# First transformer of a four-layer kernel: scores and P V as one run of narrow products, values as wide products, O turned in another order

## The chip, the cores and the metric

The kernel runs on one core of a Trainium2 chip. The metric is the device time of one launch in microseconds (us). Three launches of the kernel before took 3877.02, 3872.96 and 3869.68 us, with a median of 3872.96 us.

## The reference

Four layers are chained on `x` of 4 x 512 tokens with 128 features. Each layer normalises `x`, runs a mixer `s` and a gate network `g`, and adds `s * silu(g)`. The gate network of the third layer (`L2_ffn`) is a transformer of six layers with 16 heads of 64 and a window of 32 keys; it is the "first transformer" of this change. The gate network of the fourth layer (`L3_ffn`) is a transformer of two layers with 8 heads and a window of 64; it shares code with the first.

```python
def attn_layer(x, Wqkv, qs, ksc, Wo):
    qkv = x @ Wqkv
    q, k, v = jnp.split(qkv, 3, -1)
    ...
    q = l2norm(q) * qs
    k = l2norm(k) * ksc
    q = q * cos * scale + rotate_half(q) * sin * scale
    k = k * cos * inv + rotate_half(k) * sin * inv
    out = local_attention(q, k, v)
    return out @ Wo
def local_attention(q, k, v):
    bk2, bv2 = (look(bk), look(bv))
    sim = jnp.einsum('bhwie,bhwje->bhwij', bq, bk2) * QK_SCALE
    sim = jnp.where(mask, -jnp.finfo(sim.dtype).max, sim)
    attn = jax.nn.softmax(sim, -1)
    return jnp.einsum('bhwij,bhwje->bhwie', attn, bv2)
```

`look` puts a block of 32 keys behind the block before it, so each block of 32 queries sees 64 keys. Each layer is followed by a feed-forward layer (norm, 128 to 2 x 341, GELU gate, back to 128).

## The kernel before

All matrices are fp32, with features on the 128 partitions and tokens along the row. `transformer` (line 705 on) runs three generators side by side: `queries_keys` (q and k of one batch row and one half of the heads), `attention`, and `feed_forward`. A batch row of a layer is a "row" here: six layers by four batch rows are 24 rows in the first transformer, and each row has two slots, one for each group of eight heads. `merge` (line 949) draws from the three generators by hand-written weights. Each `yield` names a cost, and the generator that has done the smallest share of its weight goes next. That fixes the order in which the program issues work; a scheduler behind it may still move an instruction whose inputs are late. [...]

A slot of attention has two units, `j` = 0 and 1, each with four heads, that is 16 blocks of 32 queries by 4 heads. A unit goes through these steps in `class _Transformer`:

- `scores` (line 1380 on): two wide bf16 products put the mask into a PSUM tile, then 64 narrow products (line 1402: 64 rows by 32 columns of the array, 64 keys) add q k. After half of them, a `yield` lets the other generators in, and `turn` of the unit before is issued. VectorE then takes the row maximum (line 1415), subtracts it in two instructions (line 1419) and, after ScalarE's exponential (line 1424), sums the rows (line 1426) and takes the reciprocal (line 1428).
- `turn`: eight transposes bring P into a PSUM tile and ScalarE copies it out as `PT` (line 1440).
- `weigh`: 64 narrow products P V in two halves with a `yield` behind each; VectorE divides in two instructions (line 1473) into `On`.
- `turn_back`: eight transposes, and ScalarE copies the result in two instructions (line 1493) into `OT`. After the second unit of a slot four wide products with `Wo` follow (`l_OT,l_wo`), and VectorE adds to `y` (line 1533).
- `values`, once for each slot and one slot ahead: 16 products of 64 array columns by 256, in two halves of eight at different places, each copied out by ScalarE (line 1365) into `vo`; four DMAs on SP's queue (line 1369 on) make `ve`, a second copy in which every other block is shifted by one block.

`PS` is a pool of four PSUM tiles, two banks each, that all three generators share (`S2()` and `M()`). q and k come from four wide products for each group (`l_wqk`) that ScalarE squares (line 1304) and VectorE multiplies by the tables twice (lines 1306 and 1308); POOL adds (lines 1305 and 1309); two wide products (`sqp`), a logarithm and an exponential give the unit length, and VectorE multiplies (line 1333); eight DMAs on SP's queue rearrange each tile.

In the profile an fp32 product shows as two matmul records, wide or narrow.

Of the kernel before, what the change touches and what calls it, by code (L numbers as in the profile page):

```python
# [16 lines left out]
F32 = mybir.dt.float32  # L17
BF16 = mybir.dt.bfloat16
AF = mybir.ActivationFunctionType
ALU = mybir.AluOpType  # L20
AX = mybir.AxisListType
# [3 lines left out]
B, S, D = 4, 512, 128  # L25
NTOK = B * S
NT = S // 128
# [11 lines left out]
class Net:  # L39
    def __init__(self, tc, ctx, a, out):  # L40
        self.tc, self.nc, self.a, self.out = tc, tc.nc, a, out
        self.ctx, nc = ctx, self.nc
        self.pool = lambda name, bufs=1, **kw: tc.tile_pool(name=name, bufs=bufs, reuse_waits="tile", **kw)
        enter = ctx.enter_context
        self.keep = enter(self.pool("keep"))
        self.small = enter(self.pool("small", 4))

        core = self.keep.tile([128, 384], F32, name="core")
        nc.scalar.dma_start(core, a["k_core"])
        self.ident = core[:, 0:128]  # L50
        self.mean = core[:, 128:256]
        self.flip = core[:, 256:384]
        self.cen = self.keep.tile([128, 128], F32, name="cen")
        nc.vector.tensor_tensor(self.cen, self.ident, self.mean, ALU.subtract)
        self.eps = self.keep.tile([128, 1], F32, name="eps")
        nc.vector.memset(self.eps, 1e-5)
        self.xn = self.keep.tile([128, NTOK], F32, name="xn")
        self.turn = 0
# [648 lines left out]
    def transformer(self, pre, depth, heads, window, consts):  # L707

        with ExitStack() as stack:
            pool = lambda name, bufs=1, **kw: stack.enter_context(self.pool(pre + name, bufs, **kw))
            pools = [pool("ps", 4, space=PSUM)]

            pools += [pool("c", side="right"), pool("tab", 3, side="right"), pool("w", side="right")]
            pools += [pool("qk", 4), pool("v", 2), pool("p", 2), pool("t", 2)]
            t = _Transformer(self, pre, heads, window, pools, consts)
            t.exp_tables()  # L720
            rows = [(l, b) for l in range(depth) for b in range(B)]
            passes = t.queries_keys(rows), t.attention(rows), t.feed_forward(rows)
            slots = len(rows) * t.GP
            for i in range(slots + t.GP + 2 + t.lag):
                run = []
                if i < slots:
                    run.append((until_none(passes[0]), 10.3))
                if 0 < i <= slots + 1 + t.lag:
                    run.append((until_none(passes[1]), t.attention_weight))
                if i >= t.GP + 2 + t.lag:  # L730
                    run.append((until_none(passes[2]), t.feed_forward_weights[i % t.GP]))
                merge(run)
# [448 lines left out]
class _Transformer:  # L1181
    def __init__(self, net, pre, heads, window, pools, consts):
        self.net, self.nc, self.a, self.pre = net, net.nc, net.a, pre
        self.heads, self.W, self.inner = heads, window, heads * 64
        self.GP = heads // 8
        self.NB = 128 // window
        self.split = self.NB == 4
        self.PS, C, self.TB, self.WT, self.QK, self.VP, self.PP, self.TP = pools
        nc, a = self.nc, self.a
        self.T = 4 if self.split else 2  # L1190
        self.NU = self.T * 64 // window
        self.cols = net.load(C, a[pre + "cols"], name=pre + "_cols")
        k = net.load(C, a[consts][:, 0:256], name=pre + "_k", queue=nc.scalar)
        self.ones, self.cen = k[:, 0:128], k[:, 128:256]
        self.tiny = C.tile([128, 1], F32, name=pre + "_tiny")
        nc.vector.memset(self.tiny, 1e-36)
        n = NT // self.T
        self.mask = C.tile([128, n, 512], BF16, name=pre + "_mask")
        nc.gpsimd.dma_start(self.mask, a[consts][:, 256 : 256 + 512 * n].rearrange("p (t n) -> p t n", t=n))
        self.identb = C.tile([128, 128], BF16, name=pre + "_identb")  # L1200
        nc.vector.tensor_copy(self.identb, net.ident)

        self.ve = [C.tile([128, self.NU, 1024 // self.NB], F32, name=f"{pre}_ve{i}") for i in range(2)]
        for i in range(2 if self.split else 1):
            for lo, hi in self.second():
                nc.gpsimd.memset(self.ve[i][lo:hi, 0, :], 0.0)
        self.made, self.shift, self.weights = {}, {}, {}

        self.attention_weight = 20.4 if self.split else 25.0
        self.feed_forward_weights = (7.7, 1.7) if self.GP == 2 else (9.4,)  # L1210


        self.lag = 1 if self.split else 0
        self.y = net.xn
# [367 lines left out]

def _constants():
    f = np.float32
    p = np.arange(128)[:, None]
    c = {}
    c["k_core"] = np.concatenate([np.eye(128), np.full((128, 128), 1.0 / 128), np.eye(128)[::-1]], 1)
    i, j, n = p % 32, np.arange(32)[None], np.arange(64)[None]  # L1590
    own, before = np.where(j <= i, 0.0, MASKED), np.where(j > i, 0.0, MASKED)
    odd = p // 32 % 2 == 1
    band = np.where(odd, np.concatenate([before, own], 1), np.concatenate([own, before], 1))
    first = np.where((p < 32) & (n >= 32), MASKED, band)
    lmask = [np.where(n <= (q * 128 + p) // 8, 0.0, MASKED) for q in range(NT)]
    c["k_l0_masks"] = np.concatenate([first, band, band, *lmask], 1)
    hm = (p // 8 == np.arange(16)[None]).astype(f)
    quarter = (p % 32 // 8 == np.arange(4)[None]).astype(f)
    hl = (p % 64 // 8 == np.arange(8)[None]) * f(0.125)
    c["k_l0"] = np.concatenate([hm, quarter, hl], 1)  # L1600
    tri = np.where(np.arange(128)[None] <= p, 0.0, NEG)
    c["k_causal"] = np.concatenate([np.zeros((128, 384)), -tri], 1)
    c["k_diff"] = np.concatenate([np.where(np.arange(128)[None] <= p, 0.0, MASKED), (p % 32 == 8).astype(f)], 1)
    c["k_half"] = (p // 16 % 2 == np.arange(2)[None]).astype(f)
    for name, t in (("l2", L2F), ("l3", L3F)):
        w = t["window"]
        ones = np.kron(np.eye(4), np.ones((32, 32)))
        cen = np.eye(128) - 1.0 / 128

        block, i = np.arange(128) // w, np.arange(128)[:, None] % w  # L1610
        j = np.arange(w)[None]
        mask = np.zeros((128, NT, 2, 2, w), f)
        for q in range(NT):
            for blk in range(128 // w):
                rows = block == blk
                own, before = (0, 1) if blk % 2 == 0 else (1, 0)
                mask[rows, q, :, own] = np.where(j <= i, 0.0, MASKED)[rows][:, None]
                seen = (j >= i) & (q + blk > 0)
                mask[rows, q, :, before] = np.where(seen, 0.0, MASKED)[rows][:, None]
        c["k_" + name] = np.concatenate([ones, cen, mask.reshape(128, -1)], 1)  # L1620
        c["k_rot_" + name] = _rotary(w // 2, w)
    return {k: np.ascontiguousarray(v, dtype=f) for k, v in c.items()}
# [32 lines left out]
    return np.stack(out, 1)  # L1655


def _halves(w, heads, even_first):

    n = heads * 64
    h, r, d = np.arange(heads // 4)[:, None, None], np.arange(4)[None, :, None], np.arange(32)[None, None]
    order = []
    for g in range(heads // 4):
        for i in range(2):
            for half in range(2):
                order.append((i * n + (4 * g + r) * 64 + 32 * half + d).reshape(-1))
    v = 2 * n + np.arange(n).reshape(heads // 8, 8, 64)
    for part in v:  # L1670
        order += [part[0::2].reshape(-1), part[1::2].reshape(-1)] if even_first else [part.reshape(-1)]
    return w[:, :, np.concatenate(order)]


def _layout(i):
# [19 lines left out]
    for pre, src, names in (  # L1695
        ("l2", "L2_ffn_", ("Wqkv", "Wo", "W1", "W2")),
        ("l3", "L3_ffn_", ("wqkv", "wo", "w1", "w2")),
    ):
        for dst, n in zip(("Wqkv", "Wo", "W1", "W2"), names):
            a[pre + dst] = i[src + n]  # L1700
        a[pre + "Wqkv"] = _halves(a[pre + "Wqkv"], (L2F if pre == "l2" else L3F)["heads"], pre == "l2")
        a[pre + "cols"] = _columns(*(i[src + n] for n in ("q_scale", "k_scale", "ln_g", "ln_b", "b1", "b2")))
    a["L3_attn_A"] = i["L3_attn_A"]

# [22 lines left out]
```

## Time and profile before

| What | Value |
|---|---|
| median of three launches | 3872.96 us |
| lowest, highest | 3869.68, 3877.02 us |
| span of the profiled execution | 3866.4 us |
| TensorE busy | 3490.9 us, 90% |
| VectorE busy | 2476.9 us, 64% |
| ScalarE busy | 1847.0 us, 48% |
| POOL busy | 1161.2 us, 30% |
| mean granted TensorE clock | 0.946 |
| first transformer | from 1566 us to 3330 us of the span |

The span runs from the first to the last instruction of one execution; it is 6.6 us below the median of the launches. The first transformer's last feed-forward instructions of each row (line 1579) stand 71.0 us apart in most rows (1925.4, 1996.4 and 2067.4 us, for example), and 72.5 to 76.1 us where a new layer begins. The busy share of TensorE is built from modelled ends, so the start of one group of products and the start of the next tell more than a duration.

### The profile page before, as it was taken

The numbers are of one execution on the slowest core, as the hardware profiler recorded it, in microseconds if no ns is written. First come the engines' busy times: TensorE is split into PE (matmuls) and PEld (weight loads), VectorE is DVE, ScalarE is ACT, GpSimd is POOL, SyncE is SP. The second block draws the span as 40 slices with busy tenths as digits, with TensorE's granted clock in tenths as the row PEclk, the third lists the DMA queues.
The fourth block names the chain that finished last, engine by engine and source line by source line (L and its number), as shares of the span: only waits on it lengthen the run. The fifth ranks groups of instructions, "written<-read, shape, count | busy, mean of one in ns | idle before, by whom it ended". The sixth has DMA issues, their size and how long they took to land.

```text
span 3866.4 us, 105326 instructions
## 1 busy us (share of the span) xinstructions
PE 3490.9 (90%) x46789; PEld 1892.2 (49%) x46917; DVE 2476.9 (64%) x3429; ACT 1847.0 (48%) x2508; POOL 1161.2 (30%) x994
## 2 busy tenths in 40 slices
PE   6886999899899999899999999999999999778887
PEld 4554455444444443454555555555555555445444
DVE  6675555411553351677888888888888887367765
ACT  3333666623133334455555555555555555445555
POOL 1001344400021113443443443443443342042220
PEclk7677999999899999999999999999999999889998
DMA  1000000001000000444334444444444434322221
GB/s 39 8 24 24 8 1 1 1 30 52 2 1 3 3 1 2 116 99 117 95 94 122 96 96 120 95 99 117 98 99 103 103 88 98 110 63 69 53 49 42
DMA packets 123574, 236.12 MB, mean 61 GB/s; under 512 B 29624, under 2 KB 44128, under 8 KB 117728
## 3 DMA queue, kind: packets, MB, share of 16 engines
q1 hardware_dynamic: 114064, 209.58, 22.1%
q10 hardware_dynamic: 8624, 19.29, 1.6%
q8 instruction: 369, 6.05, 0.7%
q0 software_dynamic: 432, 0.51, 0.1%
q14 instruction: 85, 0.70, 0.1%
HBM read 50.08 MB, written 5.54 MB: 14 GB/s over the span
## 4 chain that ended last, share of the span: by engine, by line
PE 69%; ACT 11%; DVE 9%; issue 6%; DMA 2%; POOL 2%; SPq 0%; DVEq 0%; POOLq 0%; ACTq 0%
PE S L122 45%; PE S L126 6%; PE M L122 5%; PE S L1402 4%; PE o L1104 4%; ACT l_P L581 3%; PE o L614 2%; ACT l_PT L1440 1%; DMA l_tab<-in_k_rot_l 1%; PE S L1014 1%; DVE l_mx L1079 1%; ACT l_P L1126 1%; DVE l_rot L1333 1%; PE M L741 1%; DVE l_rot L1306 1%
## 5 line engine op out<-in xcount | busy, mean ns | idle before, releaser
L1309 POOL TENSOR_TENSOR l_rot<-l_rot,rotp 128x1024 f32<-128x1024 f32 x224 | 527.5, 2364 | 285.9 <-DVE rotp L1308 219.2
L1305 POOL TENSOR_TENSOR sqp<-sqp 128x512 f32<-128x512 f32 x224 | 293.3, 1310 | 832.8 <-ACT sqp L1304 825.6
L122 PE MATMUL S<-hb,l_wqk 128*128 128x512 f32 x896 | 449.4, 621 | 36.7 <-ACT l_PT L1440 11.2
L1304 ACT ACTIVATE sqp<-S 128x1024 f32<-128x1024 f32 x224 | 229.5, 1025 | 319.2 <-PE S L122 318.0
L1333 DVE SCALAR_TENSOR_TENSOR l_rot<-S,l_rot 128x1024 f32<-128x1024 f32 x224 | 262.9, 1211 | 65.3 <-ACT S L1330 37.4
L1306 DVE TENSOR_TENSOR l_rot<-S,l_tab 128x1024 f32<-128x1024 f32 x224 | 272.1, 1215 | 50.0 <-ACT sqp L1304 46.6
L126 PE MATMUL S<-core,l_P 128*128 128x128 f32 x1856 | 265.2, 287 | 38.9 <-ACT l_P L1424 16.4
L126 PEld LDWEIGHTS S<-core,l_P 128*128 128x128 f32 x1856 | 215.0, 146 | 136.8 <-issue 45.8
L122 PE MATMUL S<-l_KT,l_QT 32*128 32x256 f32 (+7 forms) x1536 | 247.4, 475 | 34.7 <-ACT l_P L1126 14.5
L1126 ACT ACTIVATE l_P<-S 128x1024 f32<-128x1024 f32 x160 | 156.8, 1023 | 254.9 <-PE S L122 254.1
L1308 DVE TENSOR_TENSOR rotp<-S,l_tab 128x1024 f32<-128x1024 f32 x224 | 270.5, 1208 | 1.4 <-POOL l_rot L1309 1.3
L122 PEld LDWEIGHTS S<-hb,l_wqk 128*128 128x128 f32 x896 | 158.3, 192 | 224.7 <-issue 151.6
L122 PE MATMUL S<-sqp,l_k 128*128 128x512 f32 x448 | 226.5, 623 | 19.1 <-issue 7.2
L1402 PE MATMUL S<-l_qk 64*32 64x64 f32 (+1 forms) x13312 | 221.1, 230 | 19.4 <-DMA l_qk<-l_rot 1.9
L1079 DVE TENSOR_REDUCE l_mx<-S 128x2 f32<-128x768 f32 (+1 forms) x192 | 154.9, 863 | 123.8 <-PE S L1014 123.8
L1402 PEld LDWEIGHTS S<-l_qk 64*32 64x32 f32 (+1 forms) x13312 | 168.2, 108 | 134.0 <-issue 129.6
L1130 POOL TENSOR_SCALAR_AFFINE_SELECT l_P<-l_P 128x256 f32<-128x256 f32 x256 | 99.8, 408 | 405.5 <-ACT l_P L1126 398.5
L122 PE MATMUL S<-l_wv,hb 128*64 128x256 f32 (+1 forms) x1600 | 219.1, 395 | 2.4 <-ACT l_vo L1365 1.2
L122 PE MATMUL S<-l_OT,l_wo 128*128 128x512 f32 (+1 forms) x512 | 207.1, 544 | 8.0 <-DVE ffu L1571 7.9
L1415 DVE TENSOR_REDUCE mx<-S 128x16 f32<-128x1024 f32 (+1 forms) x128 | 155.7, 1216 | 89.9 <-PE S L1402 89.8
L122 PE MATMUL S<-hb,l_w 128*128 128x512 f32 (+1 forms) x384 | 189.6, 630 | 23.5 <-DVE hb L1559 14.1
L122 PEld LDWEIGHTS S<-l_ve,l_PT 64*32 64x32 f32 (+1 forms) x6656 | 159.9, 108 | 99.2 <-issue 70.5
(360 smaller groups left out, 6544.8 us busy)
## 6 DMA issues: line engine op xcount, KB each, us to landing
l_qk<-l_rot SPq DMA_DIRECT2D x896, 128.0 KB
l_ve<-l_vo SPq DMA_DIRECT2D x112, 256.0 KB
l_ve<-l_vo SPq DMA_DIRECT2D x96, 224.0 KB
l_tab<-in_k_rot_l ACTq DMA_DIRECT2D x16, 1024.0 KB
l_wqk<-in_l2Wqkv SPq DMA_DIRECT2D x12, 512.0 KB
l_wv<-in_l2Wqkv SPq DMA_DIRECT2D x12, 256.0 KB
l_wo<-in_l2Wo SPq DMA_DIRECT2D x12, 256.0 KB
l_ve<-l_vo SPq DMA_DIRECT2D x24, 128.0 KB
```

What stands on the lines that cost most here:

```text
L122: self.nc.tensor.matmul(out, lhsT, rhs, start=start, stop=stop)
L126: self.nc.tensor.transpose(out, in_, self.ident[:n, :n])
L1079: nc.vector.tensor_reduce(mxv[:, bs, 2 * m + e, 3 - i], s[u][:, :, c : c + n], axis=AX.X, op=ALU.max)
L1126: nc.scalar.activation(P[u], s[u], AF.Exp, scale=scale)
L1304: nc.scalar.activation(sq, p, AF.Square)
L1305: nc.gpsimd.tensor_tensor(sq[:, 0, :], sq[:, 0, :], sq[:, 1, :], ALU.add)
L1306: nc.vector.tensor_tensor(t[:, g], p, tab[:, 0], ALU.mult)
L1308: nc.vector.tensor_tensor(m, p, tab[:, 1], ALU.mult)
L1309: nc.gpsimd.tensor_tensor(t[:, g], t[:, g], m[:, ::-1, :], ALU.add)
L1333: nc.vector.scalar_tensor_tensor(t[:, g], p[:, g, :].unsqueeze(1).to_broadcast([128, 2, S]), 1e12, t[:, g], ALU.min, ALU.mult)
L1402: net.nc.tensor.matmul(sv[W * bl : W * bl + W, e, t, g, :].rearrange("p (s k) -> p s k", s=2), qk[0][r, g, j, W * c : W * c + W], kw, star ...
L1415: nc.vector.tensor_reduce(mx, flat, axis=AX.X, op=ALU.max)
```

## The change

A class `_Paired` takes the place of `_Transformer` where the window is 32. `queries_keys`, `feed_forward` and the second transformer keep their code.

- The 64 score products of a unit and the 64 P V products of the unit before are issued one after the other, with no `yield` between them. Two PSUM tiles are then in use, one for each.
- `values` is four wide products (128 columns by 512), the two halves in one iteration of the loop instead of two. The weights of V are no longer permuted on the host, and the four DMAs into `ve` have other slices of about the same sizes.
- `turn_back` writes its eight transposes in the order of `OT`, so one ScalarE copy of 128x1024 takes the place of two. The tokens in `OT` are then in another order, and the addition to `y` is two instructions of 256 columns instead of one of 512.
- The subtraction of the maximum is one instruction of 1024 columns instead of two of 512.
- The exponential, the row sum and the reciprocal are issued later: the exponential behind the first piece of `values` or of the `Wo` product, sum and reciprocal behind `turn`, which now comes at the end of the unit's own iteration.
- The mask is in the new order of the blocks, and the weight of attention in `merge` is 16.1 instead of 20.4.

```diff
-            t = _Transformer(self, pre, heads, window, pools, consts)
+            t = (_Paired if window == 32 else _Transformer)(self, pre, heads, window, pools, consts)
...
-        self.attention_weight = 20.4 if self.split else 25.0
+        self.attention_weight = 16.1 if self.split else 25.0
...
+class _Paired(_Transformer):
...
+    def values(self, u):
...
+        for m in (0, 2):
+            p = self.S2()
+            for n in range(2):
+                net.mm(p[:, n, :], hb[:, 128 * (m + n) : 128 * (m + n) + 128], w)
+            yield 1.72
+            nc.scalar.copy(vo[:, m : m + 2, :], p)
+        for lo in (0, 64):
+            nc.sync.dma_start(ve[lo : lo + 32], vo[lo : lo + 32])
+        nc.sync.dma_start(ve[96:128], vo[32:64])
+        nc.sync.dma_start(ve[32:64, 1:4, :], vo[96:128, 0:3, :])
...
+    def turn_back(self, u, OT):
+        net = self.net
+        t = self.S2().rearrange("p g (x q) -> p g x q", q=128)
+        for g in range(2):
+            for th in range(2):
+                for a in range(2):
+                    net.transpose(t[:, g, 2 * th + a, :], u["On"][:, a, 2 * th + g].rearrange("p e d -> p (e d)"))
+        ov = OT.rearrange("p (g j) n -> p j g n", j=2)
+        self.nc.scalar.copy(ov[:, u["j"]], t.rearrange("p g x q -> p g (x q)"))
...
+    def attention(self, rows):
...
+                s = self.scores(qk, u["j"])
+            if last:
+                o = self.weigh(last)
+            if u:
+                self.weights_of(u, s)
+            if last:
+                self.divide(last, o)
+            if u or last:
+                yield 2.8
+            behind = None
+            if i % 2 == 0 and i + 2 < len(units):
+                behind = self.values(units[i + 2])
+            elif i % 2 and i > 2:
+                behind = self.close(units[i - 2], OT.pop(i - 2))
+            if behind:
+                yield next(behind)
+            if u:
+                self.exponentials(u)
+            if behind:
+                yield from behind
+            if last:
...
+                self.turn_back(last, made)
+                yield 0.9
+            if u:
+                self.turn(u)
+                yield 0.9
```

## The prediction

> **What bounds the kernel now.** I read the page's slices first, then the first transformer by rows, then TensorE in order of time, then the chain of waits. Busy tenths and granted clock, in 40 slices of the span:
>
> ```profile
> PE   6886999899899999899999999999999999778887
> ...
> PEclk7677999999899999999999999999999999889998
> ```
>
> In slices 17 to 34, the first transformer, TensorE is near full. Two neighbouring rows of it (71.0 us each; columns are busy us of TensorE, its weight loads, VectorE, ScalarE, POOL, then clock, DMA share, GB/s):
>
> ```profile
> 1925.40:1996.40 71.00, 68.50 (x1243) 37.98 (x1248) 59.19 (x65) 38.83 (x44) 29.57 (x18) 1.00 0.40 94
> 1996.40:2067.40 71.00, 68.50 (x1243) 37.94 (x1248) 59.07 (x65) 38.83 (x44) 29.57 (x18) 1.00 0.39 92
> ```
>
> TensorE is the bound at 96%, VectorE has 83%, so a microsecond taken from TensorE is worth nearly a microsecond until the row nears 59. TensorE in order of time (start, length, group; xN counts records, some are missing):
>
> ```profile
> 2002.67 1.98 PE L122 MATMUL S<-hb,l_wqk 128*128 128x512 f32 x4
> 2004.49 0.38 PE L122 MATMUL S<-l_mask,l_identb 128*128 128x512 bf16 x1
> 2005.02 0.86 PE L1402 MATMUL S<-l_qk 64*32 64x64 f32 x64
> 2005.81 1.12 PE L122 MATMUL S<-hb,l_k 128*128 128x512 f32 x2
> 2006.77 1.04 PE L126 MATMUL S<-core,l_P 128*128 128x128 f32 x8
> 2007.73 0.86 PE L1402 MATMUL S<-l_qk 64*32 64x64 f32 x64
> 2008.91 1.09 PE L126 MATMUL S<-core,l_On 128*128 128x128 f32 x8 [0.32 <-ACT l_PT L1440]
> 2009.84 1.02 PE L122 MATMUL S<-ffg,core 128*128 128x512 f32 x2
> 2011.16 1.98 PE L122 MATMUL S<-hb,l_wqk 128*128 128x512 f32 x4 [0.30 <-ACT l_OT L1493]
> 2012.98 3.60 PE L122 MATMUL S<-l_OT,l_wo 128*128 128x512 f32 x8
> 2016.42 1.88 PE L122 MATMUL S<-hb,l_wqk 128*128 128x512 f32 x4
> 2018.23 0.25 PE L122 MATMUL S<-l_ve,l_PT 64*32 64x64 f32 x2
> ...
> 2019.64 1.95 PE L122 MATMUL S<-l_wv,hb 128*64 128x256 f32 x16
> 2021.52 1.98 PE L122 MATMUL S<-sqp,l_k 128*128 128x512 f32 x4
> ```
>
> Here the reader is to compare starts. A wide record costs (2016.42 - 2012.98) / 8 = 0.43. The two halves of P V that happen to stand together at 2018.23 are 64 products in 1.41; a lone half of 32 takes 2005.81 - 2005.02 = 0.79. So 32 more products cost 0.62, and leaving a narrow run costs 0.79 - 0.62 = 0.17. Entering costs 2018.23 - 2016.42 - 4 x 0.43 = 0.09. The first wide group behind narrow or values products takes 0.10 more (1.82 at 2002.67 against 1.72). From the chain that ended last:
>
> ```profile
> 2007.84 1.02 ACT l_PT L1440
> ...
> 2010.04 1.08 ACT l_OT L1493 x2
> ```
>
> In this row the chain leaves TensorE mostly for such copies out of PSUM: TensorE wants one of four tiles. Over six rows (1925.4 to 2354.9) its listed waits sum to 13.6 us, 2.3 us a row.
>
> **The change, by its parts, for one row (four units).**
>
> *Narrow runs.* Four units have 16 halves; in the row from 1996.4 two pairs stand together and one half is cut in two, so 15 runs. After: 4. The products and their 0.0195 us each stay. 11 runs x (0.17 + 0.09) = 2.9 us. Before, 9 wide groups follow narrow or values products, after, 4: 5 x 0.10 = 0.5 us.
>
> *Values.* Before 4 halves x 1.88 (2021.52 - 2019.64) = 7.5. After 16 wide records x 0.43 = 6.9. Saves 0.6 us. ScalarE's copies and the DMAs keep number and size; the DMAs are issued half a slot earlier on SP's queue, behind the same copy (line 1365) that SP already waits for (125.6 us over those six rows) with no TensorE wait on a q/k transfer listed there. I take nothing; if the q/k transfers behind them came late, score runs would wait.
>
> *Transposes, mask, Wo product:* same counts, nothing.
>
> *ScalarE.* One 128x1024 copy at 1.01 (row of line 1440) for two at 0.59: 4 x 0.17 = 0.7 us less, hidden behind TensorE at 39 of 71 us.
>
> *VectorE.* One 128x1024 subtraction at 1.21 (row of line 1306) for two at 0.68: -0.6 a row. The addition to y, 0.65, becomes two of 256 columns; 0.42 each by the 128x256 reduction of line 1079: +0.4. Together -0.2 of 59.1, hidden. Its share becomes 59 / 67 = 88%; that is the cover that thins.
>
> *The new wait.* P V now follows the scores directly, and needs PT from ScalarE. In the middle of a slot `turn_back`, `turn`, mask, scores and P V have nothing between them by the weights. From the end of `turn_back`, PT needs at worst a square that is ahead (1.03), the OT copy (1.01) and its own copy (1.01), 3.15 with 0.1 for the handing over; TensorE has 0.87 of transposes and 1.78 of mask and scores to do. At worst 0.5 x 2 a row = 1.0, at best 0, since a q/k group (1.7) stands ahead at the slot's start. [...] ScalarE is busy 55%, so I take half: 0.5.
>
> *The waits of today.* The scores tile is held from 2004.49 to the subtraction's end at 2011.3, 6.8 us; after: 1.8 for mask and scores, 1.2 for the maximum, 1.2 for the subtraction, 4.2 us. The transposes of On no longer stand between two halves. Of 2.3 us a row I count 0.5 gone; bounds are all gone (+2.3) and twice as much (-2.3).
>
> Sum: 2.9 + 0.5 + 0.6 - 0.5 + 0.5 = **4.0 us a row**, 71.0 to 67.0. Some 21 rows run at the full pace: 84 us. Filling and draining the pipeline, three rows' worth where TensorE idles by a fifth, give half: 6 us. Span 3866.4 - 90 = 3776; the profiled span is 6.6 below the median of the launches, so **3783 us**.
>
> [...] In the middle of a slot 16 transposes, the mask and 128 narrow products will stand together: 1.74 + 0.53 + 2.75 = 5.0 us without a wide fp32 product. Two stretches of the trace, the first made of transposes, narrow products and the end of one wide product:
>
> ```profile
> 1935.40:1938.80 3.40, 3.08 (x82) 2.54 (x81) 1.22 (x2) 1.61 (x2) 0.72 (x1) 1.00 0.37 84
> 1938.80:1942.20 3.40, 3.10 (x9) 1.28 (x8) 3.37 (x5) 3.14 (x5) 0.00 (x0) 1.00 0.87 202
> ```
>
> The granted clock behind it stays 1.00, so I charge nothing. [...]
>
> **Rivals.**
>
> *The run does not stay whole (0.12).* The scheduler cuts it where PT is late, as it cuts a half of the scores today between 2041.8 and 2045.2. With 8 runs a row, 4 x (0.26 + 0.10) = 1.4 is lost, 2.6 us a row stay: 58 us, 3815. Against: P V halves do join today where nothing stands between.
>
> *VectorE eats half (0.08).* At 88% its queue is late more often; waits double, 2.3 more a row, 1.7 stay: 38 us, 3835. For: SP and TensorE already wait for line 1333. Against: it idles 12 us a row.
>
> *The waits vanish as well (0.08):* 1.8 us more a row, 5.8 x 22.5 = 130 us, 3743.
>
> *Slower: PSUM starves behind each run (0.11).* The run takes two of four tiles at once, and both hang on one VectorE burst: maximum 1.2, subtraction 1.2, two divisions 1.35. In the two tiles left TensorE can do two q/k groups, 3.4 us, behind 1.25 of P V: 4.7 in all from the scores' end. With one q/k group's two multiplications (2.4) ahead on VectorE the scores tile is free after 4.8: no stall. With two groups ahead (4.8) it is 7.2: 2.5 us x 4 = 10 a row, a net loss of 6.0, 24 rows: 3873 + 144 = 4017. It decides from 1.0 us a run, that is from 3.4 us of backlog. For: today's waits are for PSUM tiles. Against: each half's maximum at 2008.76 today starts as soon as the scores end, after 2.31 us of idleness on VectorE.
>
> *Nothing is measured (0.03):* waits give back the 4.0.
>
> **How the numbers follow.** Forecast 0.58 at 3783, by itself 3755 to 3810 (about 1.2 us a row either way). Within 0.2% (7.7 us, about what a measurement of this kernel can tell from no change) I put 0.03; slower by more 0.11; faster 0.58 + 0.12 + 0.08 + 0.08 = 0.86. The range from 3735 to 3845 leaves out the slower case, no change and the ends of the others.
>
> **What would show it.** Right: narrow runs of 128 products in one piece, about 2.75 us from first start to the next group; four a row; the values as wide records of 0.43; rows 67 us apart; VectorE about 59 us a row. The forecast is wrong if the rows stand 70 us apart or more, if TensorE's waits for PT, for On or for VectorE's tiles exceed 4 us a row, or if the clock falls below 1.00 in slices that now show 9.

## The result, and the profile after

Four launches of the changed kernel took 4054.91 to 4074.94 us, with a median of 4063.34 us, beside 3874.99 us for the kernel before (one launch more than in the table above): a ratio of 1.0489, 95% interval 1.0457 to 1.0520. The change makes the kernel 4.9% slower, 188 us, where 90 us less was forecast. The profiled execution has a span of 4053.2 us.

The slices of the page, in the order TensorE, VectorE, granted clock, and the instruction queue's line from the list of DMA queues:

```profile
PE   7887999899899988888888888888888888778887
...
DVE  6674555314435324777776777677777767457675
...
PEclk7677999999899999999998999999999999889999
...
q8 instruction: 361, 5.91, 0.6%
```

VectorE's line before was:

```profile
DVE  6675555411553351677888888888888887367765
```

TensorE falls from 9 to 8 in nearly the whole of the first transformer, and VectorE from 8 to 7: neither is full. Two neighbouring rows (us, then busy us of TensorE, weight loads, VectorE, ScalarE, POOL, then clock, DMA share, GB/s) and two stretches inside the second:

```profile
2028.65:2107.90 79.25, 69.30 (x1196) 38.10 (x1199) 58.20 (x63) 37.88 (x40) 29.24 (x19) 0.96 0.38 89
2107.90:2193.38 85.48, 69.64 (x1196) 38.38 (x1199) 62.08 (x68) 37.98 (x40) 29.45 (x19) 0.94 0.44 111
2156.39:2163.53 7.14, 0.23 (x16) 0.07 (x6) 1.77 (x3) 2.34 (x2) 0.00 (x0) 0.73 0.56 139
2163.53:2166.60 3.07, 3.07 (x42) 1.82 (x43) 2.90 (x4) 0.00 (x0) 0.00 (x0) 0.51 0.40 90
```

A row takes 79 to 85 us, not 71. In the stretch from 2156.39 no engine does much for 7 us, and behind it TensorE runs at half clock (0.51). The order of time on TensorE there (records of one run of narrow products, with lines left out):

```profile
2153.66 0.38 PE L122 MATMUL S<-l_mask,l_identb 128*128 128x512 bf16 x1
2154.18 1.43 PE L1623 MATMUL S<-l_qk 64*32 64x64 f32 x124
...
2156.34 0.24 PE L122 MATMUL S<-l_ve,l_PT 64*32 64x64 f32 x1
2156.39 0.23 PE L122 MATMUL S<-l_vo,l_PT 64*32 64x64 f32 x2
2163.53 0.31 PE L122 MATMUL S<-l_ve,l_PT 64*32 64x64 f32 x2 [6.91 <-issue]
2163.54 0.32 PE L122 MATMUL S<-l_vo,l_PT 64*32 64x64 f32 x2
```

The score run and the first three quarters of P V go at full pace, and then TensorE stops inside P V, for 7.1 us. No semaphore is waited for ("issue"), and P V's inputs had been used by the products just before. The group of P V products in 16 rows, before and then after (busy us and mean ns, then idle time ahead of them and what ended it):

```profile
L122 PE MATMUL S<-l_ve,l_PT 64*32 64x64 f32 x4096 | 100.0, 224 | 0.3 <-issue 0.2
```

```profile
L122 PE MATMUL S<-l_ve,l_PT 64*32 64x64 f32 x4096 | 105.5, 232 | 64.3 <-issue 52.2 <-ACT l_PT L1647 11.5
```

And TensorE's waits over the same 16 rows of the kernel after (us in total, times, longest):

```profile
PE S L122 <- issue: 89.1, 33, 6.9
PE S L1623 <- issue: 18.2, 18, 2.6
PE S L122 <- DVE l_rot L1333: 17.9, 16, 1.5
PE S L122 <- DVE hb L1558: 15.5, 16, 2.2
PE S L122 <- ACT l_PT L1647: 11.5, 28, 0.6
```

The products are nearly as fast as before (232 ns beside 224); the time is in front of them, and most of it has no releaser. What ends these pauses is not a semaphore but a transfer of instructions. The page counts 45637 matmuls and 45765 weight loads on TensorE and 361 packets of its instruction queue: 253 instructions to a packet of 16 KB (5.91 MB in 361); with TensorE's waits and the other instructions of its queue, which the page leaves out of its counts (92403 records in the trace), it is 256. A narrow fp32 product is two weight loads and two matmuls, so a run of 128 products is 512 instructions, two packets, in 2.5 us. In the trace, 74 pauses of over 0.5 us between two products of a run end within 2 us of such a packet's landing (the middle half of them 1.36 to 1.48 us behind it); they sum to 168 us. The kernel before has 10 such pauses, 13 us, when those that end behind a packet between any two products are counted too; 4 of them stand inside a run. For every kernel of this study (pauses of the first transformer, counted in this wider way; runs a row as counted in 16 rows, where counted; the last column is the shortest distance between the starts of two instruction transfers between 1640 and 3250 us):

```
kernel                       time us   runs a row  pauses, us   shortest distance us
before                        3873        15.2       10,  13        3.47
after                         4063         7.0       74, 168        3.33
e1  scores, yield, P V        4001                   81, 133        3.24
e2  four pieces               4033                   73, 123        3.34
e3  before, halves joined     3925                   36,  58        3.62
e4  96 products               4011                   30,  65        3.69
e5  no ve                     3992         4.0      110, 225        3.27
e6  order of before           3932        15.8       16,  18        3.40
e7  after, bf16               3778         4.0        9,  13        4.21
e8  e6, Wo later              3970        16.8       16,  28        3.45
e9  before, bf16              3707        13.8        8,  11        3.35
e10 runs of 64 apart          3999         9.8       25,  50        3.44
e11 e6, weight 20.4           3874        15.4        9,  12        3.39
e12 e7, no maximum            3631         4.0       15,  22        3.40
e13 after, no maximum         3999         6.2       69, 165        3.31
e14 before, no maximum        3855        15.2       11,  16        3.41
e15 e9, no maximum            3692        14.0        8,  11        3.42
e16 e10, no maximum           3933        10.0       25,  32        3.35
e17 e16, weight 19            3862         8.0       26,  43        3.27
e18 e16, weight 22            3914         8.8       42,  78        3.33
```

In twenty kernels no two instruction transfers start less than 3.2 us apart. But this shortest distance is not what the pauses wait for. In the 74 pauses of the changed kernel, the packet that ends the pause starts 3.8 to 18.4 us behind the one before it, 12.7 us in the median. The packet comes late.

Where TensorE stops shows this best. Count all of TensorE's instructions from the start of the trace, with weight loads and waits. In e13 (the changed kernel without the row maximum, below) all 63 such pauses inside runs stand where this count is 193 more than a multiple of 256: always at the end of one packet's instructions. The same number comes out for all 103 of e5, all 30 of e3 and 76 of the 77 of e1. Counted so, no packet of these four kernels starts while more than 303 instructions that have landed are still to run, however slow the work before it. The medians of e13's 63 pauses, from the first of the last 256 instructions at hand: TensorE has used them up after 1.35 us; the next packet starts after 1.12 us and has landed after 2.39 us; TensorE goes on after 3.86 us. A narrow run takes 256 instructions in 1.25 us, so it can empty what is at hand; in the kernel before, where most runs are of 32 with slower work between them, 10 pauses remain in the whole first transformer.

To see what each cause has, I went through all neighbouring matmuls of 16 rows and compared their distance with the usual one for such a pair (0.43 us behind a wide record, 0.0097 behind a narrow one, and so on). What is over was put to the pause, where a packet had landed 0.9 to 1.75 us ahead; to half clock, where the granted clock was below 1; or to a wait, where a semaphore ended it. In us a row:

| | row | pauses | half clock | waits | all else |
|---|---|---|---|---|---|
| before | 71.9 | 0.2 | 0.1 | 2.6 | 69.0 |
| after | 80.3 | 7.4 | 2.5 | 4.6 | 65.8 |
| difference | +8.4 | +7.1 | +2.4 | +2.0 | -3.1 |

24 rows of 8.4 are 202 us, against 188 measured.

### The profile page after: what moved, and what is told of

It reads as the page before. It is cut to its first block, busy times and chain, and to the rows that moved or that the text cites. A ratio compares the mean times of both kernels' runs of the same rounds, so it can differ in the third digit from the quotient of the medians.

```text
span 4053.2 us, 103084 instructions
## 1 busy us (share of the span) xinstructions
PE 3496.4 (86%) x45637; PEld 1895.3 (47%) x45765; DVE 2459.8 (61%) x3381; ACT 1824.1 (45%) x2412; POOL 1152.6 (28%) x992
## 3 DMA queue, kind: packets, MB, share of 16 engines
q8 instruction: 361, 5.91, 0.6%
## 5 line engine op out<-in xcount | busy, mean ns | idle before, releaser
L122 PE MATMUL S<-hb,l_wqk 128*128 128x512 f32 x896 | 461.1, 632 | 28.9 <-DVE hb L90 9.8
L122 PE MATMUL S<-l_ve,l_PT 64*32 64x64 f32 (+1 forms) x6656 | 199.0, 233 | 92.8 <-issue 71.5
L122 PE MATMUL S<-l_KT,l_QT 32*128 32x256 f32 (+7 forms) x1536 | 246.9, 474 | 34.7 <-ACT l_P L1126 14.5
L122 PEld LDWEIGHTS S<-hb,l_wqk 128*128 128x128 f32 x896 | 169.1, 200 | 228.1 <-issue 177.5
L1329 ACT ACTIVATE S<-S,l_tiny 128x1024 f32<-128x1024 f32 x112 | 121.9, 1088 | 304.9 <-issue 156.4
L122 PE MATMUL S<-l_wv,hb 128*128 128x512 f32 x448 | 220.1, 614 | 40.2 <-DVE l_rot L1333 28.5
L122 PE MATMUL S<-l_vo,l_PT 64*32 64x64 f32 (+1 forms) x6656 | 201.0, 234 | 55.3 <-issue 55.3
```

What stands on the lines that cost most here:

```text
L122: self.nc.tensor.matmul(out, lhsT, rhs, start=start, stop=stop)
L1329: nc.scalar.activation(p, p, AF.Ln, bias=self.tiny)
```

## The experiments

Eighteen kernels ran. Each time is a median beside the kernel before on the same chip.

### How the run is cut

**e1** puts a `yield` between the scores and P V.

```diff
                 s = self.scores(qk, u["j"])
-            if last:
-                o = self.weigh(last)
...
                 self.weights_of(u, s)
+                yield 1.4
             if last:
+                o = self.weigh(last)
                 self.divide(last, o)
```

> The changed kernel with other work let in between the 64 score products and the 64 P V products; nothing else is moved. Theory (TensorE runs out of instructions inside a narrow run: all 74 pauses over 0.5 us without a wait in the changed kernel's runs end 1.2 to 1.6 us after a 16 KB instruction transfer has landed, 168 us in sum): a run of 64 products is half as many instructions, so pauses fall to 15 to 40 and the time to 3840 to 3960 us. Rival (the new order starves PSUM or VectorE): both tiles and the burst are nearly as before, the time stays above 4000 us.

Measured: 4001.13 us, ratio 1.0319 (1.0269 to 1.0368), 81 pauses of 133 us. Pauses and time miss the theory, which counted the length of a run, and the time just meets the rival's mark. The count of instructions gives a reason: one group of 1.7 us between the halves is few instructions and little time. In its 77 pauses inside runs, TensorE used the last 256 instructions up in 2.43 us and went on 3.71 us behind the first of them (medians).

**e2** cuts it in four pieces of 32.

```diff
-                s = self.scores(qk, u["j"])
+                s = self.S2()
+                self.scores(qk, u["j"], s, 0)
+                yield 1.2
+                self.scores(qk, u["j"], s, 1)
...
+                yield 0.9
...
+                self.weigh(last, o, 0)
+                yield 0.9
+                self.weigh(last, o, 1)
```

> The changed kernel with the run cut in four pieces of 32 products, other work let in between; wide values, the one copy and the one subtraction stay. Theory: as in the kernel before, hardly a pause (under 8), and wide values keep their 1.0 us a row: 3835 to 3875 us. Rival (order, VectorE or late values): above 3950 us.

Measured: 4033.16 us, 1.0400 (1.0358 to 1.0443), 73 pauses of 123 us. The edit did not do what it was for: the yields were too small to let much in, and 39 runs of 128 products, 29 of 96 and 24 of 64 remain beside 57 of 32. It tells nothing of pieces that stand apart.

**e3** goes the other way: the kernel before with its halves joined to runs of 64.

```diff
-            if last and t == T // 2:
+            if last and t == T // 2 and not self.split:
...
-            if self.split and t % 2:
-                yield 1.24
+            if self.split and t == 3:
+                yield 2.48
+                if last:
+                    yield from self.turn(last)
```

> The kernel before with each unit's scores as one run of 64 and P V as another, all else as it was. Theory: 15 to 40 pauses against 4, the saved entries and exits (7 runs a row x 0.26 us x 24 = 44 us) are eaten: 3850 to 3960 us. Rival (only the changed kernel's order is at fault): no pauses, 3825 to 3840 us.

Measured: 3925.00 us, 1.0121 (1.0092 to 1.0150), with 36 pauses of 58 us. Longer runs bring the pauses into the old kernel too, with none of the other edits. Not all of the loss is theirs: TensorE's waits for PT grow as well, from 12.2 to 38.6 us in 16 rows.

**e4** leaves out 32 of the 64 score products of a unit.

```diff
-        for t in range(2):
+        for t in range(1):
```

> The changed kernel without 32 of the 64 score products of each unit (their scores are the mask alone), so a run has 96 products. Their own time is 96 x 32 x 0.0195 = 60 us. Theory: pauses fall more than in proportion, to 40 to 50 and 80 to 110 us, and fewer windows at half clock: 3870 to 3950 us. Rival: only the 60 us go, about 4000 us.

Measured: 4010.62 us, 1.0343 (1.0297 to 1.0389). Pauses fall to 30, 65 us, but the time hardly follows, against my 3870 to 3950: it is that of the rival, about 4000. Its waits over 16 rows:

```profile
PE S L122 <- DVE l_rot L1333: 63.3, 25, 3.3
PE S L122 <- issue: 41.0, 17, 6.0
PE S L122 <- DVE l_P L1635: 34.7, 25, 2.3
```

Where TensorE pauses less, it waits for PSUM tiles that VectorE holds. There is a second limit behind the first.

### What starves TensorE: traffic, or the number of instructions

**e5** leaves out the DMAs into `ve`.

```diff
-        for lo in (0, 64):
-            nc.sync.dma_start(ve[lo : lo + 32], vo[lo : lo + 32])
-        nc.sync.dma_start(ve[96:128], vo[32:64])
-        nc.sync.dma_start(ve[32:64, 1:4, :], vo[96:128, 0:3, :])
```

> Theory (TensorE runs out of instructions inside a long narrow run, since the next 16 KB of them are asked for too late): the four DMAs into ve are left out and ve stays zero, so P V uses zeros for every other block. The DMA traffic at a slot's middle falls, so an instruction transfer may land somewhat sooner, but it is still asked for at the same place. The pauses of over 0.5 us stay at 60 to 80 in number, their sum falls from 168 to 100 to 150 us, time 3970 to 4050. Rival (the ve transfers hold the instruction transfers up, and nothing else): under 25 pauses, under 40 us, time under 3930.

Measured: 3992.05 us, 1.0292 (1.0264 to 1.0320). The time is in the range, the pauses are not: 110 of them, 225 us, more than with the traffic (its runs stand whole, 4.0 a row where the changed kernel has 7.0). So the traffic into `ve` is not the cause. Single pauses are longer beside traffic: of the 74 in the changed kernel, the 35 whose packet started behind 2 us with the DMA engines over 80% busy have a mean of 3.05 us, the 27 with engines under 30% busy 1.18. The pause of 7.1 us fell on a table load of 1 MB (line 1255) and the `ve` transfers.

**e7** keeps the order and halves the instructions: q, k, P and values in bf16 for the narrow products.

```diff
-        out = self.QK.tile([128, 2, 2, S], F32, name=self.pre + "_qk")
+        out = self.QK.tile([128, 2, 2, S], kind, name=self.pre + "_qk")
...
-        vo = u["vo"] = self.VP.tile([128, 4, 512], F32, name=self.pre + "_vo")
+        vo = u["vo"] = self.VP.tile([128, 4, 512], BF16, name=self.pre + "_vo")
...
-        u["PT"] = self.PP.tile([128, 8, 128], F32, name=self.pre + "_PT")
+        u["PT"] = self.PP.tile([128, 8, 128], BF16, name=self.pre + "_PT")
```

> The whole change with q, k, P and the values in bf16 for the narrow products: each is then one weight load and one matmul instead of two and two, so a run of 128 products is 256 instructions, one block of 16 KB, instead of two; order and run lengths stay. Theory (supply of instructions): under 40 pauses and under 60 us of them in the first transformer, against 74 and 168; half the clock's loss with them; rows of 68 to 74 us where TensorE's waits for VectorE let them, time 3750 to 3900. Rival (the length of the run or the order itself makes the pauses, whatever the instructions): 60 to 80 pauses, time over 3960.

Measured: 3777.77 us, 0.9746 (0.9717 to 0.9775). Runs of 128 products stand whole, four a row, and the pauses are gone: 9, 13 us. TensorE has 33477 matmuls, 12160 fewer than the changed kernel for the 12288 narrow products of 24 rows: one instead of two for each. The rival, that the order or the number of products by itself makes the pauses, falls. The bf16 run is half as long in time too, and less data is moved (160 MB, not 236), so e7 alone does not part instructions from these; the place where TensorE stops in e13, e5, e3 and e1 does.

**e9** is its control: the same types in the kernel before.

> The kernel before with q, k, P and the values in bf16 for the narrow products, as e7 is the changed kernel with them: it tells what the changed order is worth when it has half the instructions. Runs of 32 stay. The 512 products of a row cost about 5.0 us less: 71.9 to 67.4 a row, time 3745 to 3790. If the changed order were worth its forecast 4.0 us a row once TensorE has its instructions, e7 (3778) would be 70 to 100 us below this kernel, so this one at 3850 or more. If the waits for VectorE that e7 shows (5.5 us a row) take the whole of it, the two are within 30 us of each other.

Measured: 3706.78 us, 0.9569 (0.9539 to 0.9599), 38 us better than my range: the row is 65.4 us. So without a pause worth naming the changed order still costs 71 us. The waits of e7 over 16 rows, then of e9:

```profile
PE S L122 <- DVE l_P L1638: 68.2, 51, 2.4
PE S L122 <- ACT ffg L1555: 11.0, 16, 0.7
```

```profile
PE S L122 <- DVE l_On L1476: 28.4, 15, 1.9
PE S L126 <- DVE l_rotb L1335: 10.9, 16, 0.7
```

e7's largest wait is for the subtraction, the instruction that frees the scores' tile: 4.3 us a row.

### The other edits by themselves

**e6** takes the wide values, the one copy of O and the one subtraction, in the order of before.

```diff
+                self.scores(qk, u["j"], s, 0)
+                yield 1.24
+            if last:
+                self.turn(last)
+                yield 0.9
+            if u:
+                self.scores(qk, u["j"], s, 1)
+                yield 1.24
...
+        self.attention_weight = 20.2 if self.split else 25.0
```

> The change with the order of before: wide values, one copy of O, one subtraction, and runs of 32 products with other work between them. Theory: few pauses (under 15, under 20 us in the first transformer), the values save 0.6 us a row and the copy and the subtraction something more where they are waited for: 0.6 to 1.2 us a row, 24 rows, 3843 to 3860, ratio 0.993 to 0.997. Rival (another part of the change, values in one piece, O's order or the later addition to y, costs time by itself): over 3890, with TensorE's waits rather than pauses as the place.

Measured: 3932.35 us, 1.0148 (1.0122 to 1.0175): few pauses, but slower, and the rival's mark is met. Its largest wait, and that of e11 below:

```profile
PE S L122 <- ACT l_OT L1684: 50.1, 33, 1.9
```

```profile
PE S L122 <- ACT l_OT L1684: 10.0, 31, 0.4
```

**e8** moves the Wo products behind P V.

```diff
-                if older["j"] == 1:
-                    yield from self.close(older, OT)
...
                 self.divide(last, o)
+            if older:
+                if older["j"] == 1:
+                    yield from self.close(older, OT)
```

> e6 with the Wo products behind the unit's P V instead of directly behind the transposes of On. Theory: what e6 lost against before is the wait for the one copy of O, 50.1 us in 16 rows (3.1 a row), since nothing stood between the transposes and Wo. With P V between them it falls under 0.7 us a row, and 2.4 to 3.5 us a row come back: 3932 less 58 to 84, 3845 to 3875, ratio 0.992 to 1.000. Rival (e6 is slow by the wide values or the later addition to y): over 3900.

Measured: 3969.70 us, 1.0243 (1.0214 to 1.0271). A miss: the wait for the copy of O stays at 40 us in 16 rows. It is not Wo that waits for O's values, but whatever next wants the PSUM tile.

**e11** changes one number of e6, and with it the place of that copy in ScalarE's queue.

```diff
-        self.attention_weight = 20.2 if self.split else 25.0
+        self.attention_weight = 20.4 if self.split else 25.0
```

> e6 with one number changed: the weight of attention in merge is 20.4, as before, and not 20.2. With 20.2 ScalarE's queue has the squares, the exponential or the feed-forward's logarithm ahead of the copy of O; with 20.4 the copy comes directly behind PT in about half the cases and behind a square in the others, as in the kernel before. Theory (e6 lost its time to this order, not to the wide values, the one copy, the one subtraction or the later addition): TensorE's wait for the copy of O falls from 50 us to under 15 in 16 rows, the values' 0.6 us a row stay: 3845 to 3868, ratio 0.992 to 0.999. Rival (one of those edits costs time by itself): over 3895.

Measured: 3874.17 us, 1.0003 (0.9986 to 1.0019), the median just past my range. The four edits cost nothing measurable and bring nothing measurable. The 58 us of e6 were one weight of `merge`.

**e10** keeps runs of 64, each with wide products behind it.

```diff
-            if last:
-                o = self.weigh(last)
-            if u:
                 self.weights_of(u, s)
...
-                yield 2.8
+                yield 2.5
...
                 self.exponentials(u)
+            if last:
+                o = self.weigh(last)
+                self.divide(last, o)
+                yield 2.5
```

> The changed kernel with scores and P V of a unit as two runs of 64 products, each with 3.5 us or more of wide products before the next. Theory (TensorE gets 256 instructions in no less than about 3.4 us; 64 products are 256 instructions in 1.25 us): with wide work of over 3 us behind each run the supply keeps up, so under 15 pauses and under 20 us of them in the first transformer, no half clock. 8 runs for 15 save 7 x 0.26 = 1.8 us a row, the values 0.6: 24 rows, 58 us, 3815; with up to 1.5 us a row of new waits for VectorE, 3810 to 3855. Rival (any run of 64 products pauses, by its length): 30 or more pauses and over 3920, as in the joined kernel of before. Rival (the burst on VectorE is the larger cost): few pauses but over 3880, with waits for VectorE of over 5 us a row.

Measured: 3998.98 us, 1.0322 (1.0293 to 1.0350). Pauses fall to 25, 50 us, above the marks of 15 and 20 us. In the 19 of them inside a run the packet before had started 6.3 us or more earlier, so the distance that this kernel was built on is not what decides. The time does not fall: the second rival holds, with 7.0 us a row of waits for VectorE and POOL. Of 16 rows:

```profile
PE S L122 <- DVE rotp L1308: 39.8, 41, 2.2
PE S L122 <- DVE l_rot L1333: 38.6, 18, 6.4
```

### VectorE's hold

These kernels leave out the row maximum and its subtraction: ScalarE's exponential reads the scores from PSUM. That takes 2.4 us of VectorE from each unit and frees the tile earlier. The edit in the changed order, then in the order of before (e14, e15):

```diff
-        nc.vector.tensor_reduce(mx, sv, axis=AX.X, op=ALU.max)
...
-        nc.vector.tensor_tensor(P, sv, mx.unsqueeze(2).to_broadcast([128, 16, 64]), ALU.subtract)
+        nc.scalar.activation(P, s.rearrange("p e (n k) -> p (e n) k", k=64), AF.Exp, scale=8.0)
```

```diff
+            for e in range(2):
+                nc.scalar.activation(Pv[:, e], s[:, e, :].rearrange("p (n k) -> p n k", k=2 * W), AF.Exp, scale=8.0)
```

**e12** (e7 with it):

> e7 without the row maximum and its subtraction: ScalarE's exponential reads the scores from PSUM itself. VectorE loses 2.4 us a unit, 9.6 us a row, and the scores' tile is free after one ScalarE instruction. Theory (what e7 loses against e9 is the hold of the scores' tile by VectorE's burst): the waits for line 1638's successor vanish, 4.8 us a row and a part of the half clock with them, 3640 to 3700, at or below e9's 3707. Rival (the changed order loses it at other places): waits move to the copies of ScalarE or to line 1335, and the time stays over 3735.

Measured: 3630.56 us, 0.9373 (0.9349 to 0.9396), 147 us below e7 and 76 below e9, a little better than my range.

**e13** (the changed kernel with it, fp32):

> The changed kernel, in fp32, without the row maximum and its subtraction (ScalarE's exponential reads PSUM). It parts the two limits: VectorE loses 9.6 us a row and the scores' tile its long hold, while the instructions of TensorE stay. Theory (supply of instructions first): 65 or more pauses and 140 us or more of them stay in the first transformer, the waits for VectorE (about 4 us a row, 60 to 90 in all) go: 3950 to 4015. Rival (the hold by VectorE is behind the pauses as well, or the larger cost): under 40 pauses, under 3900.

Measured: 3998.76 us, 1.0323 (1.0308 to 1.0338), in the theory's range. The pauses stay, 69 of 165 us. The waits do not all go: in 16 rows those for line 1333 shrink from 17.9 to 6.6 us and those for line 1558 from 15.5 to 12.1, while those for line 1308 grow from 3.4 to 9.4:

```profile
PE S L122 <- issue: 87.0, 36, 6.2
PE S L1623 <- issue: 21.6, 14, 2.7
PE S L122 <- ACT l_PT L1644: 12.3, 17, 0.8
PE S L122 <- DVE hb L1558: 12.1, 16, 2.3
PE S L122 <- DVE rotp L1308: 9.4, 4, 2.4
PE S L122 <- DVE l_rot L1333: 6.6, 4, 1.9
```

**e14** (the kernel before with it):

> The kernel before without the row maximum and its two subtractions (two exponentials from PSUM in their place). It waits for VectorE only about 1.1 us a row, so of 9.6 us of VectorE's work taken out nearly nothing is seen: 0 to 1.2 us a row, 3845 to 3875. If VectorE were a near bound of this kernel, as its 83% suggests, it would be under 3830.

Measured: 3855.19 us, 0.9958 (0.9943 to 0.9973). In the old order VectorE's hold costs little.

**e15** (e9 with it):

> e9 without the row maximum and its subtractions: beside e12 it tells what the changed order is worth with both limits taken away. e9 waits for VectorE 3.7 us a row, of which I let 2 to 3 go: 3635 to 3665 if the waits go, 3665 to 3690 if ScalarE's two exponentials take half of it back. Theory (the order does save TensorE time, and the two limits took more than that): this kernel 20 to 80 us above e12's 3631. Rival (the order saves nothing whatever stands around it): within 15 us of e12 or below it.

Measured: 3691.66 us, 0.9540 (0.9524 to 0.9556), 2 us past my range and 61 above e12, as the theory has it. With these the two orders can be set beside each other with each limit in place or weakened:

| narrow products | order of before | order of after | difference |
|---|---|---|---|
| fp32 | 3873 | 4063 | +190 |
| fp32, no maximum | 3855 | 3999 | +144 |
| bf16 | 3707 | 3778 | +71 |
| bf16, no maximum | 3692 | 3631 | -61 |

With both limits weakened the changed order, with the other edits of the change, saves 61 us, 2.5 us a row. fp32, with its doubled instructions, costs it 119 us with VectorE's burst (190 - 71) and 205 without it (144 + 61). The burst costs it 46 us in fp32 and 132 in bf16. The two losses overlap; that VectorE catches up while TensorE pauses would explain it, but was not tested by itself.

**e16** puts e10 and the missing maximum together, in fp32, and **e17** and **e18** give it other weights of attention, 19.0 and 22.0 for 20.5.

> e10 (two runs of 64 products apart, fp32) without the row maximum and its subtraction: both limits weakened without bf16. e10's row of 77.6 us has 7.6 of waits, 1.6 of pauses and 1.6 at half clock; the rest is 66.9. Theory (VectorE's burst makes e10's waits): waits fall to 2 to 3.5 a row, pauses stay at 1 to 2.5, half clock 0 to 1: rows of 70 to 74 us, 3830 to 3925. At 3850 or below it beats the kernel before and e14 (3855), and the order is worth something in fp32 too. Rival (e10's waits come from its order of issue): over 3950, with the waits for lines 1308 and 1333 still over 5 us a row.

> e16 with the weight of attention at 19.0 instead of 20.5, which moves two q/k groups and a unit length relative to the narrow runs. In e16 TensorE waits 2.9 us a row for line 1308 and 1.3 for line 1333, as in e10, though VectorE has 9.6 us less to do: so the waits come from the order in which q/k groups and unit lengths are issued. Theory: another weight moves them by 1 to 3 us a row, 3860 to 3960; at 3850 or below the forecast saving would be shown in fp32. Rival (those waits belong to runs of 64 whatever the weight): within 15 us of e16's 3933.

> e16 with the weight at 22.0: a full unit length and the values stand between the mask and the score run, the q/k groups are nearly as in e16. Theory: 3880 to 3960 by the same reasoning; rival: within 15 us of e16's 3933.

Measured: e16 3932.70 us, 1.0168 (1.0154 to 1.0182), just above the theory's range and below the rival's; e17 3862.14 us, 0.9973 (0.9958 to 0.9987); e18 3914.22 us, 1.0105 (1.0088 to 1.0122). The weight alone moves the same products by 71 us. Over some 16 rows the waits for line 1308 are 42.3 us in e16, 38.9 in e17 and 11.6 in e18, those for line 1333 are 20.3, 0.2 and 26.5: which of them stands lies in the order of issue, and e17 gains at line 1333 and at the values' copy (line 1601, 14.5 us in e16, none in e17), not at line 1308. No fp32 kernel with runs of 64 or more came out below e14's 3855; whether some order would, stays open. The fastest kernel that keeps fp32 is e14, with e17 close to it, and e12 with bf16 narrow products is the fastest of all. Both leave the row maximum out.

## Why the prediction was wrong

**The step that failed** is a half sentence in the part on narrow runs: "The products and their 0.0195 us each stay." That price was read off runs of 32 and of 64 products and then used for runs of 128. It is a price for products whose instructions are there. 128 of them are 512 instructions in 2.5 us, and a packet brings 256. Where TensorE comes to the end of those that have landed, the next packet is late: in e13's pauses the last 256 were used up in 1.35 us, and TensorE went on 3.86 us behind the first of them (medians). The pauses cost 7.1 us a row, more than all that was to be saved, and neither the sum nor a rival had a term for them. e7 shows it from one side (half the instructions, 9 pauses), e3 from the other (longer runs in the old kernel, 36 pauses), and e13 without VectorE's burst (69 pauses). The row was forecast 4.0 us shorter and came out 8.4 longer: of these 12.4 us the pauses are 7.1, the half clock 2.4, the waits 2.0, and 0.9 are savings that did not come.

**The savings** were 4.0 us a row in the forecast for runs, first wide groups and values; the accounting finds 3.1. The runs did not become four a row but 7.0, since the scheduler cut about half of them (98 pieces of 64 products beside 47 whole runs): the first rival was right in this, and it was not what decided. In e7, where the runs are whole, all but pauses, clock and waits is 1.5 us a row less than in e9.

**The values, the copy, the subtraction**: nothing taken for the last two, 0.6 us a row for the first. e11, which has all of them, is at 1.0003; its row is 71.6 us against 71.9, about half of the 0.6.

**The new wait for PT** was sized about right: waits for PT are 0.8 us a row where 0.5 was counted, between 0 and 1.0. The kernel before has 1.0 us of them, ahead of q/k groups and the transposes of On.

**"The waits of today"** went the wrong way: from 2.6 to 4.6 us a row where 0.5 less was counted. VectorE and POOL end 3.2 of them after, 1.1 before. The prediction named VectorE's 88% as the cover that thins, but gave its thinning a price in two rivals only, and none in the sum.

**The slower rival** (PSUM starves behind each run, 4017 us) has the right sign and a time near the measured one, mostly by another mechanism; that it comes so near is luck. Its own mechanism is real: in e7 the wait for the subtraction is 4.3 us a row, 1.1 us a run, just above the 1.0 from which it was to decide, not 2.5. Taking the burst away there brings 147 us.

**The clock** was charged nothing; 2.4 us a row of half clock came. In the changed kernel the clock falls where TensorE stands still, as in the stretch from 2156.39 (0.73 in it, 0.51 behind it): all 20 stretches at half clock in its 16 rows begin in a stop of 2.1 us or more, or within 1.6 us behind one; 17 of these stops end without a semaphore, 3 with a wait for VectorE. That transposes and narrow products lower the clock by themselves is not shown: in e12 16 transposes, the mask and a bf16 run stand in a row for 3.8 us, with no half clock in its 16 rows, but the changed kernel has no such stretch of the prediction's 5.0 us without a pause.

**Counts**: VectorE's work fell by 0.7 us a row (2476.9 us busy to 2459.8) where 0.2 was said, and ScalarE's fell by 1.0 us a row (1847.0 to 1824.1) where 0.7 was said. Of the signs of failure named, two showed: rows 70 us apart or more, and the clock. The waits for PT and for VectorE's and POOL's tiles came to 4.0 us a row, the mark itself.

In the changed kernel TensorE stops 74 times for 0.5 to 7.1 us until a packet has landed. The kernel before has 10 such pauses in its 24 rows, and e7, with the same runs in half the instructions, has 9.

## What to carry to other kernels

Before short products are put together, count their instructions against time: here a run of small fp32 products used up the last 256 instructions at hand in 1.35 us, and the next came 3.86 us after the first of them. Work between such runs is not only a cost, it is the time in which the next instructions come (e10, with wide products between runs of 64, has 25 pauses for 74); fewer instructions for the same work (bf16 products, one matmul instead of two) took nearly all pauses away (9 are left in e7). An idle stretch that the profile puts down to "issue", in the middle of products that share their inputs, is the sign to look for, and two orders should be compared at more than one weight before either is judged, since 0.2 of a weight was worth 58 us.

## What the hardware showed that was not expected

No instruction transfer of TensorE starts within 3.2 us of the one before in any of twenty kernels (3.24 us in e1 is the shortest, between 1640 and 3250 us), and TensorE goes on 1.36 to 1.48 us after one has landed (the middle half of 74). The instruction queue stands among the DMA queues of the page, and pauses had a mean of 3.05 us where the DMA engines had been over 80% busy, and 1.18 where under 30%. No packet of e13, e5, e3 or e1 starts with more than 303 instructions still to run, so TensorE's instructions are not brought far ahead, though the transfers at the pauses of the changed kernel were 12.7 us apart in the median. Why that is so, and why no two transfers came closer, was not measured. That two half measures (shorter runs in e4, spaced runs in e10) cut the pauses by more than half and left the time within 65 us of the changed kernel was the other surprise. The waits for VectorE in these two (e4's lines 1333 and 1635, 98.0 us in 16 rows; e10's lines 1308 and 1333, 78.4) suggest that the pauses had been giving it time to free PSUM.
